# The lead of a convolution and quantised-FFN kernel in another order, and weights before tables in its two-block stage

## The chip, the cores and the metric

The kernel runs on one core of a Trainium2 chip. The metric is device time in microseconds (us): the median of three runs. Before the change it is 1068.9 us (1068.55 to 1068.94).

TensorE (PE) multiplies matrices, VectorE (DVE) and ScalarE (ACT) work element by element, GpSimd (POOL) does the rest, and SyncE (SP) issues most transfers from the chip's memory. "L622" is line 622 of the kernel before the change.

## The reference, cut to what matters

```python
def conv(u, length, log_dt, C, log_A_real, A_imag, D):      # u: 32 batches, 64 heads, 1024 positions
    mask = (jnp.arange(Lq) < length[:, None]).astype(u.dtype)
    u_m = u * mask[:, None, :]
    kernel = _get_kernel(log_dt, C, log_A_real, A_imag, Lq)   # 2 Re sum_n Cs exp(dtA l), one per head
    y = jnp.fft.irfft(jnp.fft.rfft(u_m, n=2 * Lq) * jnp.fft.rfft(kernel, n=2 * Lq), n=2 * Lq)[..., :Lq]
    y = y + u_m * D[:, None]
    return y * mask[:, None, :]

def ffn(x, ...):                                            # gate, up, down: 4-bit weights
    x2 = x.reshape(-1, H)                                     # 2048 tokens of 1024
    Wg, Wu, Wd = dequant_gptq(...)                            # q * s[g] - (z[g] + 1) * s[g], groups of 128 rows
    gate = x2 @ Wg                                            # 1024 -> 2752
    up = x2 @ Wu
    return ((gate * jax.nn.sigmoid(gate) * up) @ Wd).astype(jnp.float16).reshape(B, S, H)

return x + ffn(conv(x, ...))
```

A token of the FFN is one batch and one head, and its 1024 values are the positions of the convolution's output.

## The kernel before

**Blocks.** The 64 heads are cut into four blocks of 16 heads, so of 512 tokens. Each block passes the convolution and then gate, up and down.

**Convolution.** The impulse response of a group of heads (6, 10 or 8 of them: 0 to 5, 6 to 15, 16 to 23, 24 to 31, ...) is made in steps. `head_coefficients` makes the constants of heads. `decays` (or `decay_tables`, L948 for heads 24 to 31) makes exponentials on ACT; `tables` makes sines and cosines (lines 183 to 211: some DVE steps, then ACT at L207 and L209); `factors` multiplies them (L213 to L223, DVE). `make_kernel` (L422) is a small product on TensorE (L427, L428) into `kq`, split into two f16 halves `kb` by ACT (L431) and DVE (L433), and stored by two DMAs to `kpad` in the chip's memory (L435). `toeplitz` (L518, DMA at L529) reads it back as a 128-row Toeplitz tile `t0` per head; the early tiles lie in memory that later serves others (names `w`, `ihl`, `t` in the profile). `conv_load` (L503) loads the input `u` of four heads and splits it into `uh` (ACT, L511) and `ul` (DVE, L514); `conv_split` (L495) does the split alone, for inputs fetched before. `conv_head` (L535) gives TensorE 24 matmuls a head (L552), then, for each pair of heads, masks the result on DVE into `y` (L564), rounds it to `xh` on ACT (L567) and takes the rest `xl` on POOL (L569), for the last pair of a block on DVE. Steps of `conv` are counted by `i`: eight to a head.

**FFN.** Weights are unpacked on the chip, one piece at a time (`unpack`, L576): a load by SP (L582), its zero points (L583), shift and mask on DVE (L588), two additions on POOL (L594), two casts to fp8 on DVE (L603), or on ACT for the first three pieces (L600). Pieces 0 to 20 (`w`) and `wmix` hold gate and up, twelve pieces `wd` hold down. A matmul sums one group of 128 rows into PSUM (L691, L692 in `gu_pair`; L668, L669 in `gu_one`; L746, L747 in `dn_pair`), each with an f16 high and low half of x, and after each group the sum in PSUM is rescaled by the ratio of two groups' scales (`scale_ratios`, L405 to L419), by DVE (L622, L641) or by ACT (L624, L644), so that the next group can be added.

**Stages.** The lead makes the first kernels and runs `conv(0)`, the convolution of block 0, in a loop that issues other work at given steps (`events`, L965, and the lists after it). Its generators are `unpack_it` (weights), `group_it` (tables, factors and kernel of heads 24 to 31), and the functions `kernel_6`, `ratios_gu`, `load_16`. Then `roll` (L790) runs the stages: 0 (gate and up of block 0 for four column pieces, with block 1's convolution `second_it` beside it), 1 (the same for block 1), 2, called the two-block stage (`gu_pair` on blocks 0 and 1 together, from piece 4 on, with the kernels of heads 32 to 47 put between its products by `kernel_item`), 3 and 4 (down of blocks 0 and 1, with the convolutions of blocks 2 and 3 beside), 5 (gate and up of blocks 2 and 3), 6 and 7 (down).

**Who goes first.** The program keeps estimates of when each engine is free (`td`, `ta`, `tp`). By them it chooses the engine of each rescale (`on_dve`), and it issues side work only while `room()` holds. `sides` lists the side generators of each stage with a rate of credit per step; those earlier in the list are asked first. A generator not yet done when its result is needed is run at once (`forced`). `third_it` makes constants, tables and factors of heads 32 to 47.

**Queues.** The order written in the program is kept on each engine except where a priority is given (`high_priority`) or an order is forced (`after`): each engine works in order, and SP issues the loads in order. In the lead SP issues, after the tiles of block 0: w2, z2, w3, z3, u of head 16, w4, z4, then tiles 16 to 21. w3 goes out ahead because `drain` (L858) starts the piece after next at the first step of a piece.

Of the kernel before, what the change touches and what calls it, by code (L numbers as in the profile page):

```python
# [16 lines left out]
AF = mybir.ActivationFunctionType  # L17
ALU = mybir.AluOpType
# [11 lines left out]
KSCALE = 64.0  # L30
PLACES = {("a", "pair"): 1, ("a", "single"): 2, ("b", "pair"): 3}
MAGIC = 12582912.0
RATES = {"first": (0.5, 4.6), "fill": (1.0, 0.8), "third": 0.5, "late": 0.5, "convs": 1.9}
# [131 lines left out]
def decay_tables(nc, pool, co, cst, h0, nh):  # L165
    xd = pool.tile([128, nh, 64], F32, name=f"xd{h0}")
    for h in range(nh):
        last = nc.scalar.activation(xd[:, h, :], cst[:, 0:64], AF.Exp, scale=co["na"][:, h0 + h:h0 + h + 1])
    return xd, last
# [78 lines left out]
def every(gen):  # L248
    for _ in gen:
        pass  # L250
# [8 lines left out]
class Core:  # L259
# [162 lines left out]
    def make_kernel(self, pool, h0, nh, place):  # L422
        nc = self.nc
        e1, e2 = self.fac[h0]
        q = self.psum("kq", place)[:32, 0, :32 * nh].rearrange("p (h n) -> p h n", n=32)
        for h in range(nh):
            nc.tensor.matmul(q[:, h, :], e1[:, h, :], e2[:, h, :], start=(h == 0), stop=False, skip_group_check=True)  # L427
        nc.tensor.matmul(q[:, :, 0], self.cst[0:1, 76:108], self.dm[h0 // 16][:, h0 % 16:h0 % 16 + nh, 0], start=False, stop=True,  # L428
                         skip_group_check=True)
        kb = pool.tile([32, 2, nh, 32], F16, name="kb", bufs=2)  # L430
        self.mark("act", nc.scalar.activation(kb[:, 0], q, AF.Copy, scale=KSCALE))  # L431
        self.marks["kh", h0] = self.marks["act"]
        self.mark(("kb", h0), nc.vector.scalar_tensor_tensor(kb[:, 1], q, KSCALE, kb[:, 0], ALU.mult, ALU.subtract))  # L433
        for k in range(2):
            (nc.scalar if h0 < 24 else nc.sync).dma_start(  # L435
                self.kpad[h0:h0 + nh, k, 128:].rearrange("h (a b) -> a h b", b=32), kb[:, k])
        self.known.update(range(h0, h0 + nh))

    def taps(self, pool, h0):
# [95 lines left out]
    def conv_head(self, hh):  # L535
        nc = self.nc
        h = hh % 16
        for k in range(hh, hh + 4):
            if k // 4 not in self.us and k < 64 and (k // 16 == hh // 16 or hh >= 32):
                self.us[k // 4] = self.conv_load(4 * (k // 4))  # L540
        for k in range(hh, hh + (16 if hh < 16 else 6 if hh < 32 else 3)):
            if k not in self.t0 and (k // 16 == hh // 16 or hh >= 32) and k in self.known:
                self.t0[k] = self.toeplitz(k)
        uh, ul = self.us[hh // 4]
        t0 = self.t0[hh]
        if h % 2 == 0:
            self.cq = self.psum("cq")[:, 0].rearrange("p (c h b) -> p c h b", h=2, b=B)
        q = self.cq
        for d in range(8):
            self.pe(40 * (8 - d))  # L550
            for k, (lw, uu) in enumerate(((0, uh), (0, ul), (1, uh))):
                nc.tensor.matmul(  # L552
                    q[:, d:, h % 2, :], t0[:, lw, 128 * d:128 * d + 128], uu[:, 0:8 - d, h % 4, :],
                    start=(d == 0 and k == 0 and h % 2 == 0), stop=(d == 7 and k == 2 and h % 2 == 1),
                    skip_group_check=True,
                )
            yield
        if h % 2 == 1:
            ts = slice(32 * (h - 1), 32 * (h + 1))
            y = self.cv.tile([128, 8, 2, B], F32, name="y", bufs=2)  # L560
            yv = y.rearrange("p g h b -> p g (h b)")
            xh, xl = self.x[hh // 16 % 2]
            with self.tc.high_priority(offset=100), nullcontext():
                masked = nc.vector.tensor_tensor(y, q, self.mask.unsqueeze(2).to_broadcast([128, 8, 2, B]), ALU.mult)  # L564
                self.mark(("y", hh), masked)
                self.mark("dve", masked)
                self.mark("act", nc.scalar.copy(xh[:, :, ts], yv))  # L567
                split = nc.vector if h == 15 else nc.gpsimd
                split.tensor_tensor(xl[:, :, ts], yv, xh[:, :, ts], ALU.subtract)  # L569
            self.act(570, self.dve(680, self.tp + HOP) + HOP)  # L570
# [282 lines left out]
def tile_ssm_ffn(ctx, tc, io):  # L853
    nc = tc.nc
    c = Core(ctx, tc, io)
    keep = c.keep

    def drain(gens):  # L858
        for u, ahead in zip(gens, gens[2:] + [None, None]):
            for n, _ in enumerate(u):  # L860
                if n == 1 and ahead is not None:
                    next(ahead)
                yield

    unpacks = [c.unpack_gu(i) for i in (*range(NI - 1), NI, NI - 1)] + [Later(c.unpack_dn, k, part) for part in range(3) for k in range(4)]
    unpack_it = c.unpacking = drain(unpacks)

    c.take = c.scratch([c.ihl])
    kg_stack = ExitStack()
    kg = kg_stack.enter_context(tc.tile_pool(name="kg", bufs=1))  # L870
# [22 lines left out]
    xd = decay_tables(nc, kg, co, c.cst, 0, 16)[0]  # L893
# [4 lines left out]
    def busy(h0, n):  # L898
        e1, e2 = (e[:, :4].rearrange("p h n -> p (h n)") for e in c.fac[h0])
        for _ in range(n):  # L900
            nc.tensor.matmul(c.psum("wq", "b")[:, 0, :128], e1, e2, start=True, stop=True)
# [3 lines left out]
    c.make_kernel(kg, 0, 6, "b")  # L905
    for h in range(6):
        c.t0[h] = c.toeplitz(h)
    busy(0, 8)
    every(c.tables(kg, 6, 10, ("e", 0)))
    c.conv_split(0, ("sq", 0), ("r", 6))  # L910
    every(c.factors(kg, 6, 10, xd[:, 6:]))
# [5 lines left out]
    def group_24():  # L917
        yield from c.tables(kg, 24, 8)
        yield from c.factors(kg, 24, 8, xd_24)
        while c.forced:  # L920
            yield
        c.make_kernel(kg, 24, 8, "a")
        yield
        kg_stack.close()
        wdp = ctx.enter_context(tc.tile_pool(name="wdp", bufs=1))
        c.wd = [wdp.tile([128, GI, 256], F8, name=f"wd{k}") for k in range(4)]
        yield

    group_it = group_24()
# [5 lines left out]
    def ratios_dn():  # L935
        c.rdn, c.ldn = c.scale_ratios(c.sdn, GH, GI, "dn", [(0, 8, 0, 128, 16.0)])

    def late_decay(h0, key):
        with c.after(key):
            xd, last = decay_tables(nc, kg, co, c.cst, h0, 8)  # L940
        c.mark(("xd", h0), last)
        return xd
# [3 lines left out]
    def decay_24(h, n):  # L946
        for k in range(h, h + n):
            nc.scalar.activation(xd_24[:, k], c.cst[:, 0:64], AF.Exp, scale=co["na"][:, 24 + k:25 + k])  # L948

    def kernel_6():  # L950
        c.make_kernel(kg, 6, 10, "b")
        xd_16 = late_decay(16, ("kh", 6))
        steps = c.tables(kg, 16, 8)
        next(steps)
        next(steps)
        with c.after(("kb", 6)):
            every(steps)
        for k in (2, 3):
            c.conv_split(k, ("xd", 16), ("r", 16))
        every(c.factors(kg, 16, 8, xd_16))  # L960

    def load_16():
        c.us[4] = c.conv_load(16)

    events = {7: kernel_6, 80: ratios_gu, 87: load_16, 75: lambda: c.make_kernel(kg, 16, 8, "b")}  # L965
    for i, _ in enumerate(c.conv(0)):
        if i in events:
            with c.after("dve" if i == 80 else None):
                events[i]()
        if i in (70, 74, 78, 82):  # L970
            with c.after(("sq", 16)):
                decay_24((i - 70) // 2, 2)
        if i in (32, 40, 48, 56, 64, 72, 104, 116, 124):
            next(unpack_it)
        if i in (80, 86, 92, 98, 104, 110):
            next(group_it)

    def second():
        with c.after("dve"):
            ratios_dn()  # L980
        for h in range(16, 22):
            c.t0[h] = c.toeplitz(h)
        for h in range(16, 32):
            forced, c.forced = c.forced, True
            while h >= 22 and 24 not in c.known:
                next(group_it)
            c.forced = forced
            yield from c.conv_head(h)

    def third():  # L990
# [21 lines left out]
    third_it = third()  # L1012
# [37 lines left out]
    def residuals():  # L1050
# [4 lines left out]

    convs_it = convs()
    second_it = second()
    sides = {
        0: [(unpack_it, RATES["first"][0], None), (group_it, 1.0, None), (second_it, RATES["first"][1], True)],
        1: [(unpack_it, RATES["fill"][0], None), (third_it, RATES["fill"][1], None)],  # L1060
        2: [(third_it, RATES["third"], None), (unpack_it, RATES["fill"][0], None)],
        3: [(unpack_it, RATES["fill"][0], None), (fourth_it, RATES["late"], False), (convs_it, RATES["convs"], False)],
        4: [(fourth_it, RATES["fill"][1], None), (convs_it, RATES["convs"], True)],
        6: [(residuals(), 1.0, True)],
# [80 lines left out]
```

## Time and profile before

| | |
|---|---|
| median of three runs | 1068.9 us |
| the profiled execution | 1069.55 us |
| its span | 1067.8 us |
| mean granted clock of TensorE | 0.993 |
| busy: TensorE, DVE, ACT, POOL | 1019.1, 804.4, 777.6, 248.4 us |
| span, two-block stage | about 180 to 410 us |
| DMA issues of t0 tiles | 48, of 512 KB each |

The span runs from the first to the last recorded instruction. In a row of the timeline the columns are the start, the duration, the engine, the line and operation, what it writes and reads, the number of instructions, and in brackets how long the engine stood idle before it and what ended that wait. In a row of a table by stretch they are the stretch, then its length, then for TensorE, its weight loads, DVE, ACT and POOL the busy time with the number of instructions, then the clock granted to TensorE (1.00 is full), the busy share of the DMA engines, and GB/s. A row of waits gives the waiting operation, the engine and line that ended the wait, the sum in us, the number of waits and the longest. Matmuls overlap: one of 512 columns is recorded with 0.38 us, but they start 0.216 us apart at full clock.

### The profile page before, as it was taken

The page shows a single profiled execution, that of the slowest core. Times are in us where ns is not written, and L with a number is a line of the kernel's source. Part 1 is how long each engine was busy: PE and PEld are TensorE (multiplying, and loading weights), DVE is VectorE, ACT ScalarE, POOL GpSimd, SP SyncE. Part 2 cuts the span into 40 slices and gives each one's busy share as a digit, 9 for nine tenths or more (in the row PEclk, how much of TensorE's full clock was granted, in tenths as well). Part 3 has the DMA queues.
Part 4 walks back from the last instruction along what each step waited for, and adds up shares of the span by engine and source line. Part 5 has one row for each costly group of instructions (what it writes and reads, how often), then busy time and mean ns, then how long its engine had stood idle before and what let it go on. Part 6 is the DMA issues. An engine that isn't in the chain of part 4 may idle for free.

```text
span 1067.8 us, 15316 instructions
## 1 busy us (share of the span) xinstructions
PE 1019.1 (95%) x5824; PEld 508.8 (48%) x5824; DVE 804.4 (75%) x924; ACT 777.6 (73%) x1033; POOL 248.4 (23%) x270
## 2 busy tenths in 40 slices
PE   2979999999899999999999999999999999999996
PEld 2857444444344445555565444444444444444442
DVE  8765788888987787886556767777787777777776
ACT  4867678787677778777777776666666667778775
POOL 0433133232332352223012102222211122102102
PEclk9989999999999999999999999999999999999999
DMA  6976321111011422568663001000000002424002
GB/s 203 316 238 216 107 79 40 40 60 40 32 57 51 140 91 104 165 178 273 183 206 119 30 20 39 21 21 20 12 20 21 20 21 61 147 80 155 33 1 79
DMA packets 52066, 99.74 MB, mean 93 GB/s; under 512 B 9492, under 2 KB 11412, under 8 KB 51992
## 3 DMA queue, kind: packets, MB, share of 16 engines
q1 hardware_dynamic: 38888, 70.09, 20.6%
q0 software_dynamic: 5280, 17.31, 4.3%
q10 hardware_dynamic: 7824, 11.37, 3.7%
q8 instruction: 45, 0.74, 0.3%
q14 instruction: 29, 0.24, 0.1%
HBM read 78.99 MB, written 19.76 MB: 92 GB/s over the span
## 4 chain that ended last, share of the span: by engine, by line
PE 80%; DVE 9%; ACT 4%; issue 3%; DMA 2%; POOL 1%; DVEq 0%; SPq 0%; ACTq 0%; POOLq 0%
PE chq L691 22%; PE chq L692 22%; PE chq L746 13%; PE chq L747 12%; PE cq L552 6%; PE chq L669 2%; PE chq L668 2%; DVE chq L622 1%; DMA t<-kpad 1%; ACT chq L624 1%; DVE v L704 1%; ACT chq L644 1%; DVE chq L641 1%; ACT sg L699 1%; PE chq L751 1%
## 5 line engine op out<-in xcount | busy, mean ns | idle before, releaser
L691 PE MATMUL chq<-xh,w 128*128 128x512 f16 x1216 | 459.6, 379 | 7.3 <-DVE chq L622 2.1
L692 PE MATMUL chq<-xl,w 128*128 128x512 f16 x1216 | 457.0, 379 | 0.0
L622 DVE TENSOR_SCALAR chq<-chq,gur 128x1024 f32<-128x1024 f32 x261 | 332.5, 1289 | 96.0 <-PE chq L692 95.4
L624 ACT ACTIVATE chq<-chq,gur 128x1024 f32<-128x1024 f32 x285 | 303.7, 1085 | 89.0 <-PE chq L692 88.4
L644 ACT ACTIVATE chq<-chq,dnr 128x512 f32<-128x512 f32 x374 | 242.7, 661 | 74.3 <-PE chq L747 68.1
L746 PE MATMUL chq<-ihl,wd 128*128 128x512 f16 x672 | 253.7, 379 | 2.2 <-DVE wd L603 0.8
L747 PE MATMUL chq<-ihl,wd 128*128 128x512 f16 x672 | 253.2, 379 | 0.0
L641 DVE TENSOR_TENSOR chq<-chq,dnr 128x1024 f32<-128x1024 f32 x128 | 156.5, 1231 | 77.5 <-PE chq L747 77.0
L692 PEld LDWEIGHTS <-w 128*128 128x128 fp8e4 x1216 | 118.5, 97 | 155.8 <-issue 20.4
L691 PEld LDWEIGHTS <-w 128*128 128x128 fp8e4 x1216 | 118.3, 97 | 147.9 <-issue 2.0
L310 POOL TENSOR_TENSOR ihl<-v,ihl 128x512 f16<-128x512 f32 x42 | 48.3, 1149 | 344.4 <-ACT ihl L633 344.4
L747 PEld LDWEIGHTS <-wd 128*128 128x128 fp8e4 x672 | 65.5, 97 | 71.2 <-issue 6.2
L746 PEld LDWEIGHTS <-wd 128*128 128x128 fp8e4 x672 | 65.4, 97 | 69.1 <-DVE wd L603 2.0
L552 PEld LDWEIGHTS <-t 128*128 128x128 f16 x1152 | 81.4, 98 | 34.2 <-DMA t<-kpad 1.3
L552 PE MATMUL cq<-uh,t 128*128 128x256 f16 (+3 forms) x720 | 91.3, 228 | 0.4 <-DMA t<-kpad 0.4
L552 PE MATMUL cq<-ul,t 128*128 128x256 f16 (+3 forms) x360 | 72.2, 228 | 0.0
L569 POOL TENSOR_TENSOR xl<-y,xh 128x512 f16<-128x512 f32 x28 | 36.4, 1298 | 145.1 <-ACT xh L567 142.7
L633 ACT CAST ihl<-v 128x512 f16<-128x512 f32 x42 | 25.9, 616 | 56.5 <-DVE v L704 53.1
L704 DVE SCALAR_TENSOR_TENSOR v<-chq,gul,sg 128x1024 f32<-128x1024 f32 x38 | 48.6, 1280 | 16.7 <-PE chq L692 7.9
L668 PE MATMUL chq<-xh,w 128*128 128x512 f16 x128 | 48.8, 384 | 4.5 <-ACT xh L567 3.1
L644 ACT ACTIVATE chq<-chq,gur 128x512 f32<-128x512 f32 x66 | 43.2, 660 | 13.6 <-PE chq L669 12.4
L310 POOL TENSOR_TENSOR spill<-v,spill 128x512 f16<-128x512 f32 x42 | 48.7, 1160 | 14.3 <-ACT spill L633 14.3
(258 smaller groups left out, 799.0 us busy)
## 6 DMA issues: line engine op xcount, KB each, us to landing
t<-kpad SPq DMA_DIRECT2D x48, 512.0 KB, 4.8
spill<-spill POOLq DMA_DIRECT2D x42, 256.0 KB, 2.3
ihl<-spill ACTq DMA_DIRECT2D x42, 256.0 KB, 2.7
z<-zc SPq DMA_DIRECT2D x29, 256.0 KB, 4.2
u<-xF SPq DMA_DIRECT2D x12, 512.0 KB, 4.4
xr<-xT SPq DMA_DIRECT2D x12, 512.0 KB, 4.7
out<-xr POOLq DMA_DIRECT2D x24, 256.0 KB, 2.9
w<-qgu SPq DMA_DIRECT2D x21, 256.0 KB, 4.0
```

Source lines behind the costliest of these rows:

```text
L310: self.nc.gpsimd.tensor_tensor(out, a, b, op)
L552: nc.tensor.matmul(q[:, d:, h % 2, :], t0[:, lw, 128 * d:128 * d + 128], uu[:, 0:8 - d, h % 4, :], start=(d == 0 and k == 0 and h % 2 == 0 ...
L622: self.mark("dve", self.nc.vector.tensor_scalar(q, q, col, None, ALU.mult))
L624: self.mark("act", self.nc.scalar.activation(q, q, AF.Copy, scale=col))
L641: self.mark("dve", self.nc.vector.tensor_tensor(q, q, cols.to_broadcast([128, 2, 512]), ALU.mult))
L644: self.mark("act", self.nc.scalar.activation(q[:, k], q[:, k], AF.Copy, scale=cols[:, k]))
L668: nc.tensor.matmul(q[:, k], lw, xh[:, g, :], start=(g == 0), stop=False, skip_group_check=True)
L691: nc.tensor.matmul(q[:, b], lw, xh[:, g, :], start=(g == 0), stop=False, skip_group_check=True)
L692: nc.tensor.matmul(q[:, b], lw, xl[:, g, :], start=False, stop=(g == GH - 1), skip_group_check=True)
L704: nc.vector.scalar_tensor_tensor(v, q, last, self.sg.pop(ct - 21), ALU.mult, ALU.mult)
L746: nc.tensor.matmul(qs[j], lw, self.ihl[:, g, 0], start=(g == 0), stop=False, skip_group_check=True)
L747: nc.tensor.matmul(qs[j], lw, self.ihl[:, g, 1], start=False, stop=False, skip_group_check=True)
```

## The change

The diff touches the lead (before `roll`) in six places and one line of `sides`:

- `make_kernel` for head 16: the two copies and the two stores get a priority of 400. Its place goes from step 75 to step 71.
- `conv_head`: the mask and split of heads 12, 13 and 14, 15 of block 0 get the priority 400 in place of 100.
- `drain`: piece 3 (w3) is not started ahead; it is started in the new event `tiles_16` at step 111, behind tiles 16 to 18, which `second` issued before.
- `busy`: 13 in place of 8 filler matmuls on TensorE ahead of the first convolution.
- `kernel_6`: one input split goes ahead of the factors of head 16, and the other behind them. The ratios of gate and up go from step 80 to step 66, behind the last factor of head 16. The decays of heads 24 to 31 go from steps 70 to 82 to steps 84 to 96, `group_it` from steps 80 to 110 to steps 100 to 120. `second` waits where it forced `group_it` before.
- `sides[2]`: `unpack_it` is asked first and `third_it` second.

No instruction is added or removed but the five fillers.

```diff
@@ make_kernel
-        self.mark("act", nc.scalar.activation(kb[:, 0], q, AF.Copy, scale=KSCALE))
...
+        with self.tc.high_priority(offset=400) if h0 == 16 else nullcontext():
+            self.mark("act", nc.scalar.activation(kb[:, 0], q, AF.Copy, scale=KSCALE))
+            self.marks["kh", h0] = self.marks["act"]
+            self.mark(("kb", h0), nc.vector.scalar_tensor_tensor(kb[:, 1], q, KSCALE, kb[:, 0], ALU.mult, ALU.subtract))
+            for k in range(2):
+                (nc.scalar if h0 < 24 else nc.sync).dma_start(
+                    self.kpad[h0:h0 + nh, k, 128:].rearrange("h (a b) -> a h b", b=32), kb[:, k])
@@ conv_head
-            with self.tc.high_priority(offset=100), nullcontext():
+            with self.tc.high_priority(offset=400 if h > 12 and hh < 16 else 100):
@@ tile_ssm_ffn
-    def drain(gens):
+    def drain(gens, held):
         for u, ahead in zip(gens, gens[2:] + [None, None]):
             for n, _ in enumerate(u):
-                if n == 1 and ahead is not None:
+                if n == 1 and ahead is not None and ahead is not held:
                     next(ahead)
                 yield
...
-    unpack_it = c.unpacking = drain(unpacks)
+    unpack_it = c.unpacking = drain(unpacks, unpacks[3])
...
-    busy(0, 8)
+    busy(0, 13)
...
-        for k in (2, 3):
-            c.conv_split(k, ("xd", 16), ("r", 16))
+        c.conv_split(2, ("xd", 16), ("r", 16))
         every(c.factors(kg, 16, 8, xd_16))
+        c.conv_split(3, ("sq", 16), ("e", 16))
+
+    def tiles_16():
+        for h in range(16, 19):
+            c.t0[h] = c.toeplitz(h)
+        next(unpacks[3])
...
-    events = {7: kernel_6, 80: ratios_gu, 87: load_16, 75: lambda: c.make_kernel(kg, 16, 8, "b")}
+    events = {7: kernel_6, 66: ratios_gu, 87: load_16, 111: tiles_16, 71: lambda: c.make_kernel(kg, 16, 8, "b")}
     for i, _ in enumerate(c.conv(0)):
         if i in events:
-            with c.after("dve" if i == 80 else None):
+            with c.after(("e", 16) if i == 66 else None):
                 events[i]()
-        if i in (70, 74, 78, 82):
+        if i in (84, 88, 92, 96):
             with c.after(("sq", 16)):
-                decay_24((i - 70) // 2, 2)
+                decay_24((i - 84) // 2, 2)
...
-        if i in (80, 86, 92, 98, 104, 110):
+        if i in (100, 104, 108, 112, 116, 120):
             next(group_it)
...
-        for h in range(16, 22):
+        for h in range(19, 22):
             c.t0[h] = c.toeplitz(h)
         for h in range(16, 32):
-            forced, c.forced = c.forced, True
             while h >= 22 and 24 not in c.known:
-                next(group_it)
-            c.forced = forced
+                yield
             yield from c.conv_head(h)
...
-        2: [(third_it, RATES["third"], None), (unpack_it, RATES["fill"][0], None)],
+        2: [(unpack_it, RATES["fill"][0], None), (third_it, RATES["third"], None)],
```

## The prediction

> **What bounds the kernel.** First the page's shares and its chain.
>
> ```profile
> PE 1019.1 (95%) x5824; PEld 508.8 (48%) x5824; DVE 804.4 (75%) x924; ACT 777.6 (73%) x1033; POOL 248.4 (23%) x270
> PE 80%; DVE 9%; ACT 4%; issue 3%; DMA 2%; POOL 1%; DVEq 0%; SPq 0%; ACTq 0%; POOLq 0%
> ```
>
> TensorE sets the end, so only its holes count. Next, which holes (view of waits, TensorE):
>
> ```profile
> PE cq L552 <- DMA w<-kpad: 4.5, 3, 2.7
> PE chq L668 <- ACT xh L567: 3.1, 1, 3.1
> ...
> PE chq L751 <- DVE chq L641: 1.3, 1, 1.3
> PE chq L669 <- DVE xl L569: 1.3, 1, 1.3
> PE chq L668 <- ACT w L600: 1.2, 1, 1.2
> ```
>
> Then where they lie (table by stretch: TensorE's busy time first, the granted clock third from the end):
>
> ```profile
> 20.48:23.89 3.41, 0.77 (x4) 0.47 (x3) 3.22 (x6) 2.90 (x5) 0.00 (x0) 1.00 0.77 223
> 23.89:27.30 3.41, 3.35 (x44) 3.27 (x44) 3.27 (x8) 0.11 (x1) 0.00 (x0) 0.64 1.02 346
> ...
> 58.90:62.40 3.50, 1.38 (x3) 0.38 (x4) 2.67 (x2) 1.81 (x2) 3.25 (x3) 0.51 1.05 404
> 62.40:65.80 3.40, 3.40 (x20) 2.49 (x19) 0.92 (x3) 1.79 (x4) 0.00 (x0) 0.50 1.06 396
> ...
> 280.00:300.00 20.00, 17.13 (x77) 7.08 (x76) 18.45 (x19) 13.66 (x15) 9.73 (x10) 1.00 0.19 66
> ...
> 700.00:1050.00 350.00, 349.85 (x1611) 156.96 (x1610) 268.29 (x232) 249.39 (x316) 55.11 (x61) 1.00 0.14 46
> ```
>
> Two places can give: 54.8 to 66, where TensorE stands and then runs at half clock, and the two-block stage and the one after it (280 to 300, 460 to 500). From 700 on nothing can be won or hidden, so a gain before it reaches the end.
>
> **The change, part by part.** The profiled execution took 1069.55 us: 1067.8 of span, 1.75 around it. The median, 1068.9, is 0.65 lower; I apply the sum to the median.
>
> *Fillers.* Eight took 3.79 us in 16 rows, 0.237 each; five more are 10 rows, 2.4 us, and end at 23.6 (21.24 + 2.4). The first Toeplitz tile comes at 23.95 by DMA, which covers them. They take away the hole after which the clock fell (0.64), so heads 0 to 5, 11.7 us long before, would take some 10.1 (six heads of 1.54 as at 39.20 to 40.74, the product of kernel 6 at 0.9). But head 6 waits for a DMA at 37.34, whose kernel comes from DVE at 28 and not from TensorE: the 1.6 us gained only widen the 1.65 us hole there to 3.2. Term 0. Without that cover they would cost 2.4. A 3.2 us hole may lower the clock in its turn: one stretch of 3.41 us at half clock is 1.7 us, and the holes before heads 8 and 9 (0.17, 0.68) take half of it: 0 to +0.9, taken as 0, since the drain below is then bound by DVE.
>
> The Trainium skill, "TensorE: Matmul & The Clock Gate", section "HAM oscillation — how this bites in real kernels", asks only that TensorE's idle gaps stay below about 3.4 us. The row disagrees: a gap of 2.71 us was followed by half clock. By the rule the fillers change nothing and the 3.2 us hole is free; by the row both matter. The sum is the same.
>
> *Kernel 16.* Its product (44.27 to 45.05, 0.78 us) moves from between the halves of head 9 to before that head, into the 0.68 us wait for its tile: conv 0 ends at about 54.1, not 54.8. Its two copies (kb 0.36 on ACT, 0.41 on DVE) go ahead of DVE's sine chain, where the second stood until 49.16. The two stores (2.00 us of issue on ACT) then leave near 44.5 and land near 50, not at 53.5 and 54.2. Behind them on ACT stand the decays, which have time now that they are moved twelve to fourteen steps later.
>
> *Loads.* SP issues in program order, and in the built program each load waits for the one eight places ahead to land; SP's issues therefore stand 1.36 us apart (45.79, 47.14, 48.48, 49.84). New order: w2, z2, u(16), tiles 16 to 18, w3, w4, tiles 19 to 21. w3 was ahead of u(16); without it one transfer of 1.36 us fewer stands before u(16): it lands near 53.9 (55.28 before). Tile 16 was issued only at 54.21, when kernel 16's second store had landed; with the store landed near 50 it follows u(16) by one place, near 55.3 (59.55 before). Pushed back: w3, to 58.7; it is used only in the next stages.
>
> *Drain of conv 0.* The order on DVE shows the ratios (L414 to L419, 2.34 of it RECIPROCAL) before the last masks:
>
> ```profile
> 52.86 2.34 DVE L418 RECIPROCAL ihl<-ihl 128x88 f32<-128x88 f32 x4
> 55.11 0.63 DVE L564 TENSOR_TENSOR y<-cq,mask 128x512 f32<-128x512 f32 x1
> ...
> 56.43 0.68 DVE L564 TENSOR_TENSOR y<-cq,mask 128x512 f32<-128x512 f32 x1
> ```
>
> In the changed order the ratios stand earlier, but four sine steps (L194, L197, L198, L200: 0.69 + 1.38 + 0.34 + 0.67 = 3.1 us) now stand between the two masks, so the last mask still comes at about 55.9 to 56.6. What is won is the rest: ul (L514) goes at 57.3, not 58.7, the last split xl ends at 60.3, not 61.6, and conv products of head 16, whose tiles are there, fill part of the wait. Clock: half until 65.8 before; TensorE is now busy from 57.3 and nearly without a hole from 59, so the stretch ending at 62.4 should lift it. Sum to the product of kernel 24, at 72.75: before, 61.63 to 65.82 at half and the rest full is 9.0 us of full-clock work; after, 7 conv products less (0.8) and two products more (0.4), 8.6, from 60.3: 1.05 until 62.4, 7.6 after it, 70.0; say 70.3. Term −2.5. If the clock stays low to 65.8: 71.7, −1.0. If the chain of casts also shortens by the 0.7 us that conv 0 ends earlier: −3.2. If xl still ends last at 61.6: 0. Late next: L223 for kernel 24, now about 69.9, 0.4 us ahead of its product.
>
> *Two-block stage: weights first.* No instruction is added. Counting in the built programs the matmuls between the last TensorE instruction that a weight's cast waits for and its first use: 8 to 23 for pieces 13, 14, 15 and 17 before, 165 or more after; for the down weights 22 to 34 before, 370 or more after. So the holes around these go:
>
> ```profile
> 282.99 0.38 PE L692 MATMUL chq<-xl,w 128*128 128x512 f16 x1
> 284.89 0.38 PE L691 MATMUL chq<-xh,w 128*128 128x512 f16 x1 [1.52 <-DVE chq L622]
> ...
> 287.78 0.38 PE L691 MATMUL chq<-xh,w 128*128 128x512 f16 x1 [0.58 <-DVE w L603]
> ```
>
> 20.00 − 17.13 = 2.9 us in 280 to 300 (a table step, L221, 1.33, and two casts, 2.89, stood ahead of rescales), and 0.63 and 1.31 at 470 and 482, of which I take 1.5: −4.4. Given back: nine more casts (L603) and half as many shifts (L588) now run before the down stage. On DVE, 187.7 of 230 us busy from 180 to 410, a cast is 0.68 alone and 1.45 beside POOL, a shift 0.48 or 0.86: 8 to 17 us more. I take +0.5 (0 to +2) for it, by the nearest row: 200 to 220, 82% busy, no hole. Tables second: the product of kernel 40 now follows L223 after a rescale, L222 and a cast (1.29 + 0.42 + 0.68 to 1.21 + 0.42 = 2.8 to 3.3), against 11 matmuls of 0.216, 2.4: +1.0 (0.4 to 1.6), the rescales behind included. Near 212 us a rescale now follows another rescale, two casts, a shift and 13 small steps of coefficients (1.28 + 2 × 0.68 + 0.48 + 13 × 0.17, the last by rows such as L130 and L113 at 0.18), 5.3 us against 24 matmuls, 5.2: +0.5 (0 to 1.5). Term −2.4 (−5 to +1).
>
> The Trainium skill's page "SBUF — State Buffer", section "Who interferes with whom", speaks against it: the port that DVE and GpSimd share is held by one for a whole instruction. By that each moved cast may lose one POOL add (0.72), 6.5 us of DVE; by the median row none.
>
> Sum: −2.5 − 2.4 = −4.9, **1064.0 us**, own range 1061 to 1067.
>
> **Rivals.** About 0.2% (2.1 us) is what a measurement can tell: 1066.8 to 1071.0 is no change.
> - The stage gives back what it won (denser DVE, kernel 40): the lead's 2.5 is left, 1066.4. For it: DVE at (187.7 + 17) of 226, 91%. Against: the slack of 165.
> - The lead gives nothing: xh, ul, xl still queue behind each other on ACT and DVE, the clock stays low: 0 to −1, with the stage 1066 to 1066.5. Both fail: no change, 1068 to 1069, as would a planner that fits the same work in as before.
> - Slower: DVE becomes the bound of the two-block stage, and a rescale comes as late as at 283 (1.52) once for each of the nine casts moved in: 13.7. 1068.9 − 6.9 + 1.0 + 13.7 = 1076.7; it decides from six such places on. For it: that wait was made by just this crowd. Against: 82% busy stretches without a hole.
>
> **Numbers.** Forecast 0.45; one of the two gains alone 0.28 (at 1066.4, just inside faster; 0.17 faster, 0.11 same); both nil 0.12; slower 0.15. Faster 0.62, same 0.23, slower 0.15. Range 1060.7 (1068.9 − 3.2 − 5.0) to 1071, where the slower case begins.
>
> **What would show it.** Clock full from 24 to 58 and no half stretch after 62.4; head 16's tile landed by 55.5; kernel 24's product near 70.3; no hole behind L603 from 280 to 300 and at 470; a hole of about 1 us before kernel 40's product. Wrong if TensorE's first long run still starts at 61.6, or if waits for DVE L622 grow past 6 us.

## The result, and the profile after

The changed kernel takes 1073.6 us in the median (1071.2 to 1076.0, nine runs), against 1069.6 us for the kernel before in the same runs: 1.0033 times as long, 95% interval 1.0024 to 1.0042 (a ratio here is worked out from all runs and is not the quotient of the two medians). The forecast was 1064.0 us. The profiled execution took 1074.7 us, with a span of 1072.9. The change adds one line above most of the code, so before's L622 is L623 in the kernel after.

The page's shares and TensorE's view of waits, after:

```profile
PE 1020.7 (95%) x5834; PEld 511.8 (48%) x5834; DVE 810.3 (76%) x925; ACT 775.2 (72%) x1029; POOL 244.8 (23%) x270
...
PE chq L692 <- DVE chq L623: 8.7, 11, 2.5
PE cq L553 <- DMA w<-kpad: 4.6, 3, 2.4
PE cq L553 <- ACT uh L512: 3.0, 1, 3.0
PE chq L692 <- DVE v L678: 2.6, 2, 2.0
PE cq L553 <- DVE ul L515: 1.5, 1, 1.5
PE chq L692 <- DVE uh L434: 1.1, 1, 1.1
```

Two of these waits before:

```profile
PE chq L691 <- DVE chq L622: 2.1, 3, 1.5
PE chq L691 <- DVE v L677: 0.6, 1, 0.6
```

TensorE works as long as before, within 2 us. It has ten matmuls and ten weight loads more, from the five fillers; DVE has one instruction more and ACT four fewer, since the planner chose another engine for some rescales. The waits have changed. Those behind weight casts (L603, and L746 for the down weights) are gone. In their place stand eleven waits for a rescale by DVE, 8.7 us against 2.1 in three waits before, one for `kb` of kernel 32 (L434, 1.1), and one of 2.0 us for the product `v` of the one-block stage (L678), far from any line that the diff touches.

The second of these stretches before:

```profile
460.00:500.00 40.00, 37.81 (x320) 23.14 (x319) 31.00 (x41) 27.93 (x47) 14.59 (x18) 1.00 0.71 220
```

The same stretches after, and two new ones (columns as before):

```profile
280.00:300.00 20.00, 19.51 (x90) 8.61 (x89) 17.44 (x21) 16.07 (x18) 10.10 (x11) 1.00 0.24 79
460.00:500.00 40.00, 39.88 (x345) 24.51 (x343) 32.07 (x39) 28.35 (x47) 11.09 (x12) 1.00 0.63 202
...
143.30:146.40 3.10, 1.07 (x5) 0.42 (x5) 0.92 (x2) 2.77 (x4) 1.70 (x2) 1.00 0.00 0
146.40:149.80 3.40, 3.40 (x9) 1.21 (x8) 2.03 (x3) 1.68 (x3) 2.32 (x3) 0.50 0.21 81
```

From 280 to 300 TensorE is busy for 19.51 us, where it was 17.13; from 460 to 500 for 39.88, where it was 37.81. So the gain that the prediction expected from weights first is there: 2.4 + 2.1 = 4.5 us of busy time, forecast 4.4. But at 144 us there is a hole, and after it 3.4 us at half clock, that before did not have. Against an ideal spacing of matmuls (0.216 us for 512 columns, counted from start to start), the profiled execution of after loses 1.4 us less than before up to 80 us, 4.3 more from 140 to 180, 4.1 more from 180 to 400, and 2.2 less from 400 to 520.

The lead. TensorE's rows, before and then after:

```profile
37.34 1.69 PE L552 MATMUL cq<-ihl,w 128*128 128x256 f16 x24 [1.65 <-DMA w<-kpad]
...
61.63 0.58 PE L669 MATMUL chq<-xl,w 128*128 128x512 f16 x1 [1.29 <-DVE xl L569]
...
72.68 0.69 PE L427 MATMUL kq<-e2t,e1t 128*32 128x32 f32 x16
```

```profile
36.99 4.83 PE L553 MATMUL cq<-ihl,w 128*128 128x256 f16 x48 [2.39 <-DMA w<-kpad]
...
57.88 0.37 PE L553 MATMUL cq<-uh,t 128*128 128x256 f16 x1 [2.96 <-ACT uh L512]
59.77 0.37 PE L553 MATMUL cq<-ul,t 128*128 128x256 f16 x1 [1.52 <-DVE ul L515]
...
71.86 0.69 PE L427 MATMUL kq<-e2t,e1t 128*32 128x32 f32 x16
```

Heads 6 and 7 take 4.83 us together, where before they took two times 1.69: here the hole before head 6, 2.39 us, was followed by half clock (37.2 to 40.6). From 59.77 on TensorE's rows follow without a hole, where that began at 61.63, and the product of kernel 24 stands at 71.86, not 72.68.

### The profile page after: what moved, and what is told of

Its sections match the earlier page's. It is cut to its first block, busy times and chain, and to the rows that moved or that the text cites. A ratio compares the mean times of both kernels' runs of the same rounds, so it can differ in the third digit from the quotient of the medians.

```text
span 1072.9 us, 15340 instructions
## 1 busy us (share of the span) xinstructions
PE 1020.7 (95%) x5834; PEld 511.8 (48%) x5834; DVE 810.3 (76%) x925; ACT 775.2 (72%) x1029; POOL 244.8 (23%) x270
## 4 chain that ended last, share of the span: by engine, by line
PE 80%; DVE 10%; ACT 4%; issue 3%; DMA 2%; POOL 0%; DVEq 0%; ACTq 0%; SPq 0%
PE chq L692 21%; PE chq L693 20%; PE chq L747 13%; PE chq L748 13%; PE cq L553 7%; DVE chq L623 3%; PE chq L669 2%; PE chq L670 2%; ACT chq L645 1%; ACT chq L625 1%; DVE v L705 1%; ACT sg L700 1%; PE chq L752 1%; DVE w L604 0%; DVE wd L604 0%
## 5 line engine op out<-in xcount | busy, mean ns | idle before, releaser
L692 PE MATMUL chq<-xh,w 128*128 128x512 f16 x1216 | 459.6, 379 | 12.5 <-DVE chq L623 6.2
L623 DVE TENSOR_SCALAR chq<-chq,gur 128x1024 f32<-128x1024 f32 x259 | 330.7, 1290 | 90.2 <-PE chq L693 88.6
L645 ACT ACTIVATE chq<-chq,dnr 128x512 f32<-128x512 f32 x368 | 239.2, 661 | 74.8 <-PE chq L748 68.8
L642 DVE TENSOR_TENSOR chq<-chq,dnr 128x1024 f32<-128x1024 f32 x131 | 160.3, 1231 | 81.4 <-PE chq L748 80.7
L570 POOL TENSOR_TENSOR xl<-y,xh 128x512 f16<-128x512 f32 x28 | 34.1, 1219 | 171.0 <-ACT xh L568 140.8
L634 ACT CAST ihl<-v 128x512 f16<-128x512 f32 x42 | 26.0, 618 | 59.3 <-DVE v L705 55.9
L595 POOL TENSOR_TENSOR w<-w,z 128x256 int32<-128x256 int32 x42 | 32.5, 795 | 90.3 <-DVE w L589 90.2
L700 ACT ACTIVATE sg<-chq,gul 128x1024 f32<-128x1024 f32 x38 | 42.3, 1113 | 10.1 <-PE chq L693 8.7
```

The lines of the kernel that those rows point to most:

```text
L623: self.mark("dve", self.nc.vector.tensor_scalar(q, q, col, None, ALU.mult))
L642: self.mark("dve", self.nc.vector.tensor_tensor(q, q, cols.to_broadcast([128, 2, 512]), ALU.mult))
L645: self.mark("act", self.nc.scalar.activation(q[:, k], q[:, k], AF.Copy, scale=cols[:, k]))
L692: nc.tensor.matmul(q[:, b], lw, xh[:, g, :], start=(g == 0), stop=False, skip_group_check=True)
L700: nc.scalar.activation(sg, q, AF.Silu, scale=last)
```

## The experiments

All ratios are to the kernel before, run beside it on the same chip; its median there was 1069.4 to 1069.8 us. Of every run one execution was traced.

| run | what it is | median, us | ratio, 95% interval |
|---|---|---|---|
| e1 | lead's edits alone, 13 fillers | 1071.4 | 1.0019 (1.0010 to 1.0027) |
| e2, e11 | swap alone, twice | 1073.9, 1073.8 | 1.0046 (1.0032 to 1.0060), 1.0033 (1.0022 to 1.0045) |
| e3 | the change again | 1074.5 | 1.0050 (1.0037 to 1.0062) |
| e4 | before, 13 fillers | 1073.7 | 1.0037 (1.0023 to 1.0050) |
| e5 | lead's edits, 8 fillers | 1068.2 | 0.9985 (0.9976 to 0.9994) |
| e6 | before, 8 fillers and 5 tiny ones | 1073.4 | 1.0040 (1.0024 to 1.0056) |
| e7 | before, 8 wide fillers | 1069.2 | 1.0001 (0.9991 to 1.0010) |
| e8 | swap, no additions on POOL | 1071.1 | one run, no interval |
| e9 | lead's edits, 8 wide fillers | 1068.1 | 0.9983 (0.9974 to 0.9992) |
| e10 | the change, 8 fillers | 1072.2 | 1.0021 (1.0012 to 1.0030) |
| e12 | swap, weights at half the rate | 1069.7 | 0.9997 (0.9988 to 1.0006) |
| e13 | before, two spill buffers | 1069.8 | 0.9995 (0.9986 to 1.0005) |
| e14 | e4 with two spill buffers | 1071.7 | 1.0021 (1.0012 to 1.0030) |
| e15 | e9 with two spill buffers | 1068.8 | 0.9991 (0.9982 to 0.9999) |
| e16 | the change with two spill buffers | 1072.0 | 1.0030 (1.0017 to 1.0043) |

### The halves, and the fillers alone (e1 to e4)

e1 is the change without the swapped line of `sides`; e2 is that line alone; e4 is the line of the fillers alone.

```diff
@@ e2, on the kernel before
-        2: [(third_it, RATES["third"], None), (unpack_it, RATES["fill"][0], None)],
+        2: [(unpack_it, RATES["fill"][0], None), (third_it, RATES["third"], None)],
@@ e4, on the kernel before
-    busy(0, 8)
+    busy(0, 13)
```

> The lead's edits alone; the two-block stage asks tables first again. Theory 1 (weights first costs in the two-block stage, the lead gains little): 1.0 to 2.5 us faster than before, ratio 0.9977 to 0.9990; TensorE's waits for the rescale L623 from 180 to 410 fall back to about 2 us, the waits behind the weight casts at 283 to 292 are back. Theory 2 (the lead's new order costs, by what it leaves to the stages after it, 140 to 180 above all): 2 to 4 us slower than before, ratio 1.002 to 1.004.

> The swap in the two-block stage alone, on the lead of before. Theory 1: 1 to 4 us slower than before (ratio 1.001 to 1.004), with waits for the rescale of about 7 us in place of 2 and no wait behind a weight cast at 283 to 292. Theory 2: 2 to 5 us faster (0.995 to 0.998), as the prediction had it for the weights.

> The changed kernel as it is, to compare with the two halves on one chip: ratio about 1.003 to before. If the two parts simply add, its difference is the sum of those of the two halves; if theory 1 and an interaction hold, the sum is off by more than 1 us. The wait at 144 us for the spill's DMA (2.0 us, then half clock) shows whether it belongs to the kernel or to one execution.

> The kernel before with 13 fillers in place of 8, nothing else. The prediction's step: the clock stays full from 24 to 28 and head 6's tile takes the gain, so within 0.1% of before. Rival: the wider hole before head 6 lowers the clock there, 0.5 to 1.5 us slower.

The lead's edits were slower, not faster as theory 1 had it; the swap was slower by 4.5 us in e2's median (theory 1 said 1 to 4), with 8.3 us of waits for the rescale. So both theories were half right, and the surprise is e4: five fillers in a hole of 2.7 us cost 0.37%, as much as the whole change. Its trace shows no loss in the lead. The time goes at 140 to 160 us (4.3 us lost there against 1.2 before) and at 640 to 660 (3.5 against 1.4). In e3 the hole at 144 us was absent, so it comes in some executions of the kernel and not in others.

What happens at 140 us in the kernel after is seen in the view of the DMA queues. Before, then after, from 139.0 to 144.6 us (packets and share by queue; then the store's issues, size, and us from issue to landing):

```profile
q0 software_dynamic: 80, 0.26, 12.2%
...
spill<-spill POOLq DMA_DIRECT2D x1, 256.0 KB, 2.4
```

```profile
q0 software_dynamic: 80, 0.26, 12.6%
q8 instruction: 1, 0.02, 1.1%
...
spill<-spill POOLq DMA_DIRECT2D x1, 256.0 KB, 4.3
```

A store of 256 KB by POOL (`spill`, the halves of a product) lands after 2.4 us before and after 4.3 us in the changed kernel, and a fetch of instructions is in the window. In the list of packets of the kernel after, 15 of the store's 16 closing 4-byte packets come at 141.1 to 141.3; the fetch, one packet of 16,384 bytes, begins at 141.5 and takes 0.97 us; the last closing packet comes at 142.5. In e3 that packet went out just ahead of the fetch, at 141.4, and the store landed after 2.8 us. The list doesn't name the DMA engine of a packet; that the late packet and the fetch share one is inferred from this order.

The fetches on this queue are TensorE's: between two of them stand 256 matmuls and weight loads on average (250 to 262 in most intervals of the quiet stage after 660 us). With 13 fillers there are ten more matmuls and ten more weight loads in front. The eighth fetch still comes after 1969 of TensorE's recorded instructions and the tenth after 2487, in e4 as in before, so both come 20 instructions earlier against the work. The ninth comes after 2241 before, at 147.3 us, and after 2221 in e4, at 142.1: 40 earlier against the work, which puts it onto the first store. Why it moved by 40 and not by 20 isn't shown.

Who waits, in the kernel after (the timelines of ACT, POOL, DVE and TensorE, one row of each):

```profile
143.60 0.62 ACT L634 CAST spill<-v 128x512 f16<-128x512 f32 x1 [1.93 <-DMA spill<-spill]
```

```profile
144.31 1.14 POOL L310 TENSOR_TENSOR spill<-v,spill 128x512 f16<-128x512 f32 x1 [4.44 <-ACT spill L634]
```

```profile
145.48 0.75 DVE L678 SCALAR_TENSOR_TENSOR v<-chq,gul,sg 128x512 f32<-128x512 f32 x1 [2.30 <-POOL spill L310]
```

```profile
146.29 0.48 PE L692 MATMUL chq<-xh,w 128*128 128x512 f16 x1 [2.03 <-DVE v L678]
```

`spill` has one buffer, so ACT's cast waits for the store, POOL's subtraction for the cast, DVE's `v` for the subtraction, and TensorE, 2.03 us, for the PSUM that `v` reads. The 3.41 us at half clock after it add 1.7.

### Is it the fetch? (e5 to e8)

```diff
@@ e5: the lead's edits, busy(0, 8)
@@ e6, on the kernel before, behind busy(0, 8)
+    e1, e2 = (e[:, :4].rearrange("p h n -> p (h n)") for e in c.fac[0])
+    for _ in range(5):
+        nc.tensor.matmul(c.psum("wq", "b")[:, 0, :4], e1, e2[:, :4], start=True, stop=True)
@@ e7, on the kernel before, busy(0, 8) with
-            nc.tensor.matmul(c.psum("wq", "b")[:, 0, :128], e1, e2, start=True, stop=True)
+            nc.tensor.matmul(c.psum("wq", "b")[:, 0, :192], e1, e2, start=True, stop=True)
@@ e8, the swap alone, and in unpack
-            nc.gpsimd.tensor_tensor(lanes, lanes, z[:, a:b].bitcast(I32), ALU.add)
+            if act:
+                nc.gpsimd.tensor_tensor(lanes, lanes, z[:, a:b].bitcast(I32), ALU.add)
...
-                    nc.vector.tensor_scalar(dst[:, a:b], raw[:, a:b], -64.0, None, ALU.add, saturate=False)
+                    nc.vector.tensor_scalar(dst[:, a:b], raw[:, a:b], -8.0, None, ALU.add, saturate=False)
```

> The lead's new order with 8 fillers as before, and tables first. Theory F (the fillers cost nothing where they stand; their 20 more TensorE instructions move the 16 KB fetches of its instructions, and a fetch then meets POOL's store at 140 us): the fetch stays near 145 to 147 us and the gain of the lead's order is kept, 0.5 to 2 us faster than before, 2 to 4 us faster than with 13 fillers. Rival W (the wider hole and the clock around head 6 cost, or the lead's new order itself): within 1 us of the run with 13 fillers, so 1 to 3 us slower than before.

> The kernel before with 8 fillers and, behind them, five more of 4 columns each: the number of instructions of 13 fillers, but at most 0.5 us of TensorE's time, in a hole. Theory F: the fetch comes near 141 to 143 us and the time is 2 to 4 us above before, as with 13 full fillers. Rival W: within 0.7 us of before.

> The kernel before with 8 fillers of 192 columns in place of 128: about the time of 12 fillers, but the number of instructions of 8. Theory F: the fetch stays near 147 us, clock full from 24 us on, and the time is 0 to 1 us below before. Rival W: 2 to 4 us above before, as with 13 fillers.

> Weights first on the lead of before, and the two additions on POOL left out of every unpacking by DVE (the zero points are not added; a constant of 8 stands for them), so that POOL reads beside DVE only for the low halves of the products. Theory P (DVE's steps are lengthened by POOL beside them, 16 us from 180 to 410, and the denser crowd of weights first makes rescales late): DVE's lengthening falls below 8 us and TensorE's waits for the rescale from 8.3 us to 2 to 4. Rival O (it is the order: table steps and casts stand ahead of rescales, at their normal length): waits of 6 us or more stay.

Theory F holds in all three times. Five fillers of four columns, which keep TensorE busy for next to nothing, cost 0.40%; eight wide fillers, which fill the hole and keep the clock full from 24 us on, cost nothing. It is the number of instructions that counts, not the filling. The place of the fetch was forecast for e7 (147, it came at 146.6) and nearly for e6 (141 to 143, 140.7), but not for e5: there it came at 142.5, not at 145 to 147, since the lead's order moves it too. It missed the first store and came just behind the issue of the second, which landed after 3.1 us, and TensorE waited for `v` no longer than before (0.6 us). Where the fetch falls there is luck. e6 met two stores, and its view of waits shows both:

```profile
PE chq L691 <- DVE v L677: 3.0, 2, 2.4
PE chq L691 <- DVE v L704: 2.8, 3, 2.4
```

The first is the store at 139.16 (4.74 us to land, fetch at 140.7); the second is an output store at 638.4 (4.47 us, fetch at 640.1), whose buffer `v` shares. With each hole of 2.4 us came 3.4 us at half clock.

e5 is the lead as the prediction had it, and it is faster: 0.9985. Its product of kernel 24:

```profile
70.22 0.69 PE L427 MATMUL kq<-e2t,e1t 128*32 128x32 f32 x16
```

The forecast said 70.3.

e8 fell between its theories. Without the additions, DVE's instructions that overlap POOL's are 9.4 us longer (their duration less the shortest of the same form, from 180 to 410) instead of 16.0, and the waits for the rescale are 5.8 us in six instead of 8.3 in ten. So in this one trace a third of them went with POOL's additions. The largest, 2.5 us, stayed.

### The swap, and the best version (e9 to e12)

```diff
@@ e12, the swap alone, at half the rate
+        2: [(unpack_it, 0.5, None), (third_it, RATES["third"], None)],
```

> The lead's new order, tables first, 8 fillers of 192 columns: the filling of 13 with the instructions of 8. Theory F: no meeting of fetch and store at 140 us, the clock is full from 24 us on: 1 to 2.5 us faster than before, and not slower than with 8 narrow fillers (1068.2 against 1069.5). Rival: the wider hole before head 6 costs as much as the warm clock wins, within 0.5 us of the 8 narrow ones.

> The whole change with 8 fillers in place of 13. If the three parts add (lead without fillers -1.3, swap +2 by its trace or +4.5 by its time, fillers by the meeting of fetch and store +3 to +4), this lies 1 to 3 us above before. If the swap gained what the prediction said, it would lie 3 to 5 us below.

> The swap alone once more, for a second trace: its first was its fastest execution (1071.6 against a median of 1073.9). Theory: the fixed price is the 2 us in that trace (waits for rescales of 8.3 us less the weight waits), and what slower executions add is a store met by a fetch, at 140 or 640 us or another. Rival: the slower executions show more waits for rescales in the two-block stage itself.

> Weights first on the lead of before, but asked at half the rate (0.5 credits a step for 1.0), so that tables find room between them. Theory O (weights taking all the room push the table steps late and beside POOL, ahead of rescales): TensorE's waits for rescales from 160 to 410 fall from 8.3 us to 4 or less, the waits behind weight casts stay gone, and the time falls 2 to 4 us below that of the swap. Rival: waits stay above 6 us, since the same table steps and casts fit no better.

Two of the parts add: +0.33 to 0.46% for the swap and −0.15% for the lead without extra fillers make +0.2 to +0.3%, e10 measured +0.21%. The fillers bring it to +0.33 and +0.50%; so here they add 0.12 to 0.29 points, less than the 0.37 that they cost alone. The 2.5 us hole is alike in every trace of the swap at its full rate. In the kernel after, DVE and POOL stand so there:

```profile
378.97 1.29 DVE L623 TENSOR_SCALAR chq<-chq,gur 128x1024 f32<-128x1024 f32 x1 [0.28 <-PE chq L693]
380.17 1.13 DVE L218 SCALAR_TENSOR_TENSOR ul<-t,t 128x256 f32<-128x256 f32 x1
381.22 1.37 DVE L219 SCALAR_TENSOR_TENSOR uh<-t,ab 128x256 f32<-128x256 f32 x1
382.51 1.28 DVE L623 TENSOR_SCALAR chq<-chq,gur 128x1024 f32<-128x1024 f32 x1
```

```profile
379.86 1.16 POOL L310 TENSOR_TENSOR ihl<-v,ihl 128x512 f16<-128x512 f32 x1 [1.36 <-ACT ihl L634]
380.97 1.33 POOL L310 TENSOR_TENSOR spill<-v,spill 128x512 f16<-128x512 f32 x1
```

Two factors of kernel 40 stand between two rescales. Each takes 0.42 us alone; here 1.13 and 1.37. L218 ends 0.28 us after POOL's first subtraction (381.02), L219 0.29 us after the second (382.30): by these ends each waits until POOL's instruction is over. The rescale that TensorE needs comes 1.66 us later for it.

Whether that hole costs more than itself depends on where it falls. The half-clock stretches of one execution all lie on one grid of 3.413 us (in e10: 23.38, 57.52, 381.78). The two grid windows around the hole in e2, then in e10:

```profile
376.15:379.56 3.41, 1.74 (x8) 0.58 (x7) 3.41 (x3) 2.31 (x4) 2.44 (x2) 1.00 0.00 0
379.56:382.97 3.41, 2.05 (x23) 1.11 (x23) 3.17 (x6) 0.72 (x1) 0.56 (x1) 1.00 0.34 117
```

```profile
378.37:381.78 3.41, 0.90 (x5) 0.37 (x4) 3.41 (x4) 1.09 (x1) 2.34 (x3) 1.00 0.07 28
381.78:385.20 3.42, 3.42 (x22) 1.51 (x21) 1.73 (x4) 1.09 (x1) 0.00 (x0) 0.50 0.71 220
```

In e2 the hole is cut in two by the grid, TensorE is busy for 1.74 and 2.05 us of the windows, and the clock stays. In e10 it lies in one window, 0.90 us busy, and the next window runs at half. All 18 traces agree. Cut each trace by its own grid from 30 to 1040 us: in the 33 windows at full clock that a window at half clock followed, TensorE was busy for 0.14 to 1.45 us by the recorded rows, and in every full-clock window that none followed, for 1.51 us or more. e11 had this stretch too, and a store met at 144.9 us (4.2 us to land, 1.8 us of wait for ACT); together 3.5 us of the 3.7 by which its span is above e2's (1073.5 against 1069.8). Its waits for the rescale are the same, 8.5 us. So the swap's fixed price is 2 us by e2's trace, its fastest execution. Of what e11 adds to it, about half is the met store, as expected, and the other half the clock; the other executions of the swap were not traced.

At half the rate the swap costs nothing, and wins nothing: waits for the rescale are 3.2 us, those behind weight casts still gone, and other waits stand in their place (`v` 2.9):

```profile
PE chq L691 <- DVE chq L622: 3.2, 4, 1.1
...
PE chq L691 <- DVE v L704: 2.9, 4, 1.2
PE chq L691 <- ACT chq L624: 2.0, 2, 1.6
```

The 1.6 us behind ACT's rescale come from a store that was met at 144.4 us (4.0 us to land), as in e11; no half clock followed. e12 also tells order from lengthening: by the measure used for e8, DVE's instructions beside POOL are 18.6 us longer in e12, more than the 16.0 of e2, and yet the waits for the rescale fell from 8.3 to 3.2 us. So it isn't the sum of the lengthening that makes rescales late, but which steps stand ahead of them.

e9, the lead's edits with eight wide fillers, is the fastest version that ran: 0.9983, interval 0.9974 to 0.9992. It doesn't differ from e5 by more than the intervals. No run joins the lead's order with the paced swap.

### Through the one buffer? (e13 to e16)

```diff
-            hl = self.fw.tile([128, 2, 512], F16, name="spill", bufs=1)
+            hl = self.fw.tile([128, 2, 512], F16, name="spill", bufs=2)
```

> The kernel before with two buffers in place of one for the product halves that POOL stores (spill), nothing else: the control for the next run. Theory B (a store met by a fetch costs because the one buffer is not free): before meets few, so 0 to 1.5 us faster than before.

> 13 fillers and two spill buffers. Theory B: the store near 140 us may land late all the same, but nobody waits 2.0 us for it and no half clock follows; what is left is the late output store at 640 us in some executions: within 1.5 us of before, where 13 fillers with one buffer were 4 us above it. Rival: the five fillers cost elsewhere, the time stays 3 to 4 us above before.

> The lead's order, tables first, 8 wide fillers and two spill buffers: the best version so far and the buffer. Theory B: 1.5 to 3 us below before (it was 1.7 below with one buffer).

> The whole change with two spill buffers. Theory B with the swap's own price: the fillers' part goes, what stays is about what the change with 8 fillers had, 1 to 3 us above before (the holes behind rescales in the two-block stage, 8.5 us, are still there). Rival: 3.5 to 5 us above, as without the buffer.

e13, the control, is as fast as before. In e14 the store at 139.97 met the fetch and landed after 4.2 us, as in e4; with a second buffer TensorE doesn't notice. The wait for `v` of the one-block stage in e4, then in e14:

```profile
PE chq L691 <- DVE v L677: 2.5, 2, 2.0
```

```profile
PE chq L691 <- DVE v L677: 0.6, 1, 0.6
```

So at 140 us the price goes through the one buffer, and the fillers' ratio falls from 1.0037 to 1.0021, though the two intervals overlap. But e14 is still 0.21% above before, more than the 1.5 us expected: its trace shows the output store at 636 us late (3.9 us, 1.8 us of wait), and what its other executions lose was not traced. In e16 the store was late as well (4.3 us) without a hole, and the swap's waits (8.7 us) and a half stretch at 382.8 remain; its ratio cannot be told from that of the change or of e10. e15 shows no gain over e9 (0.9991, and 1.5 to 3 us were expected).

## Why the prediction was wrong

Two terms failed: the fillers' 0 and what weights first gives back. In their ratios the lead's order measured −1.6 us (e5; forecast −2.5), the fillers +4 alone (e4, e6) and +1.3 to +3.1 in the change (it and e3 against e10; forecast 0), the swap +3.5 to +4.9 (e11, e2; forecast −2.4).

**Fillers: the term of 0 failed.** The steps that led to it held but for sizes: in the change the fillers end before the first tile lands, the clock is full from 24 us, and the wait for head 6's tile takes most of the gain (it ends at 36.99, 37.34 before). The five cost 0.6 us there, not 2.4, since the last fourteen rows stand 0.11 us apart and the others 0.21, the clock having risen at 20.1; in e4, where it rose at 22.3, they cost 1.8. The wider hole before head 6 (2.4 us) was followed by half clock in three of the four traces of the lead's edits with 13 fillers; that was priced, at up to 0.9. (The hole of 0.17 us that the prediction puts before head 8 stands before head 7, by the rows at 39.20 and 40.74; the sum doesn't change.) What the working left out is that an instruction on TensorE also moves the fetches behind it: it priced the fillers by TensorE's time alone. In e4 and e6 this is about 4 us, with a chain that goes fetch, store, buffer, cast, `v`, PSUM, and half clock behind three of the four holes.

**Lead's order: right in mechanism, and its size depends on the execution.** In the kernel after, kernel 16's stores were issued at 44.6 (forecast 44.5) and landed at 50.4 and 52.3 (50); tile 16 landed at 56.2 (55.3, before 59.55). In e5, with 8 fillers, the last mask stands at 56.6, `xl` ends at 59.3 and kernel 24 at 70.2 (55.9 to 56.6, 60.3, 70.3). That the forecast was met so closely is in part luck: e10 has the same lead, and there kernel 24 comes at 71.75. The eight traces with the lead's edits fall into two halves: 70.2 to 70.8 in e3, e5, e9 and e15, and 71.4 to 72.3 in the change, e1, e16 (half clock behind head 6's wait, from 36.5 to 38.1 on) and e10 (6.8 us of half clock from 23.4 on). So in the change only 0.8 us were left at kernel 24, and of the signs that the prediction named, a full clock from 24 to 58 and none at half after 62.4, neither came: half clock stood at 37.2 to 40.6 and until 64.5 (until 62.5 in e5). Of e5's 2.5 us 1.6 reach the end in its ratio; in its trace a half stretch at 284 us, where before ran full through its weight waits, takes part of it.

**Weights first: the gain was right (4.5 us, forecast 4.4), what is given back was 2.0 and came to 6.5 or more.** The terms that failed are "+0.5 for denser DVE" and "+1.0 for kernel 40": waits for the rescale grew by 6.6 us in the change. The nearest row, 200 to 220 at 82% without a hole, doesn't say what happens when small table steps meet POOL ahead of a rescale: DVE's lengthening beside POOL rose from 9.3 us before to 16.0 in e2. And kernel 40's product was not late; the rescale ahead of it was, by two factors. Pacing (e12) shows that the order does it. The rule of "SBUF — State Buffer" in the Trainium skill, section "Who interferes with whom", that the shared port is held for a whole instruction, agrees with L218 and L219 to 0.3 us. The forecast weighed 6.5 us of DVE's time by it and put none of it on the path.

The slower rival was the true one in kind: waits for L622 grew to 8.7 us, past the 6 us that were named as the sign of error. It had nine places of 1.5 us, the trace has eleven of 0.8 on average.

**The clock.** The rule that the prediction weighed (gaps below 3.4 us are free) doesn't hold here: holes of 1.5 to 2.5 us were followed by half clock when they left TensorE busy for 1.45 us or less in one grid window. The Trainium skill's page "TensorE: Matmul & The Clock Gate", section "What's actually happening", says that the window is free-running. e2 and e10 show what that means: the same hole of 2.5 us, and in e10 1.7 us more behind it.

## What to carry to other kernels

Adding instructions to a stream, even in idle time, shifts its later fetches, so look at what transfer such a fetch can meet and whether a single buffer hangs on it; fill with wider instructions, not with more. A gap of one and a half microseconds or more should be priced with the half-clock window that may follow it, and as a chance, since the grid shifts from one execution to the next. When side work is put first on a shared engine, look for short steps that would then stand between two links of the critical chain, with the durations they have beside POOL, and pace the side work rather than letting it take all the room (here that took the cost away and won nothing).

## What the runs showed of the hardware

The instruction fetch is on no list of costs, yet it moved the time by 0.4%: one packet of 16,384 bytes takes 0.9 to 2.0 us, and a store whose last packet comes with its end or after it lands after 3.9 to 4.7 us, not 2.4. Such a meeting is no rare thing and costs only where somebody waits: before, a store at 318.2 us meets a fetch too and lands after 4.1 us, and TensorE doesn't stand. Nor is every late store a fetch: in e8 one landed after 3.7 us with other transfers beside it and no fetch. The Trainium skill, "Runtime: NRT & Kernel Launch", section "Instruction fetch mechanics", gives the block of 256 instructions that the traces show and calls the cost of a block mostly hidden. For TensorE itself it is (before, it is busy for 349.85 of the 350 us from 700 on, with 12 fetches in them), but not for the store. Half clock came behind grid windows in which TensorE was busy for 1.45 us or less, with holes as short as 1.5 us (e5, e9 and e15 at 282 to 283 us), in stretches of 3.41 us on a grid that is fixed in one execution and shifts between executions. That makes a part of the spread between runs of one kernel: 1.7 of the 3.7 us between the two traces of the swap. A DVE step of 32 columns (L105) took 1.89 us in the first trace of the swap, where it is 0.19 in the lead; in the kernel after it took 1.90 and ended at 176.22, 0.06 us after the second of two additions on POOL (174.74 to 176.16).
